# Node products moved ahead of the sums, and the sums dealt out by a tile quota, in a one-core graph kernel

## The chip, the cores and the metric

The kernel runs on one core of one Trainium2 chip. The metric is the device time of one execution in microseconds (us); lower is better. A core has five engines that take their instructions in order from queues of their own: PE (matmuls; its weight loads are listed apart as PEld), DVE and ACT (elementwise work), POOL (here almost only the issue of indirect DMAs) and SP (here the issue of plain DMAs). Line numbers such as L1353 are those of the kernel before the change.

## The reference, cut to what matters

N = 6250 nodes with 64 features, 206,250 edges (sorted by `dst`). Every edge gives a hidden row, rows are summed by node, and each node's mean goes through a small network and a layer norm:

```
msg = concat([x[dst], edge_attr])              # per edge, 128
h   = relu(msg @ W1a.T + b1a) @ W1b.T + b1b    # per edge
agg = segment_sum(h, src) / max(count, 1)      # per node
z   = relu(concat([x, agg]) @ W2a.T + b2a) @ W2b.T + b2b
out = concat([z, x]) @ Wr.T + br
y   = layernorm(x + out)
```

The second edge layer is linear, so the kernel sums `relu(...)` (128 values and a count) and applies W1b to the sums.

## The kernel before, in words

`fast_path` does all the work here; `general_path` is a second program behind a flag and does not run with these inputs.

**Blocks.** The edges are padded to 1612 tiles of 128 and taken in 124 blocks of 13 tiles (`NG`), in an order that strides through the array so that every block spreads over all nodes. The main loop (`for k, ep_ in enumerate(epoch_of)`) runs block by block. The nodes are cut into 49 bins of 128 (`NB`). In block k, PE computes the hidden rows of the block's edges (`hidden`, L1313), ACT applies the relu into one of four row buffers (`orow`, L1316), and the ranks of the edges in their bins are worked out for a later block on PE, DVE and ACT (`bins_of`, `counts_of`, `slots`), so that each row gets a slot of its own in DRAM.

**Scatters.** `scatter(k - LEAD)`, two blocks later, has POOL issue one indirect DMA (L1353) for each tile of 128 rows. In blocks 8 to 103 (`JOIN_FROM`, `JOIN_TO`) six of the 13 tiles are joined: two joins turn three tiles each into rows of four ("quads") by one-hot matmuls (`marks` on DVE L1201 and on ACT L1206 and L1207, `join` L1233, `join_rows` L1246), and each join is one indirect DMA (L1324). So such a block has 7 + 2 = 9 scatters, and each of the other 28 blocks has 13: 1228 in all. A table in `scatter` (`pace`) makes some scatters of block k wait for matmuls of block k + 2. The row buffers close the circle: ACT's copy of the low bits into the buffer (L1626, at the head of each block) waits until earlier scatters have read it.

**Sums.** Rows go to four DRAM buffers by epoch (blocks 0 to 103, 104 to 115, 116 to 119, 120 to 123), and the quads to one more. A slot range that is surely full can be read back while later blocks still run: a `Step` is the range of tiles [lo, hi) of all bins together with the block `at` which it is full. `FULL = (4, 8, 12)` and `FULLQ = (4, 8, 11)` set these ranges. `groups_of` cuts a step into groups of at most 3 bins and 12 tiles. A group is read by SP (`read`, L1415, into nine buffers, `READS`), DVE makes its one-hot tiles (`nodes_of`, L1444; this is done ahead, when the group before it is finished, by `mark`), PE sums it with one matmul of two passes per tile (`summed`, L1463), and the result is added into `part` (DVE L1523; the first time ACT copies it, L1521). In block k the first group that was issued in an earlier block is summed half ahead of the last part of the hidden rows and half after the joins; further groups follow at the end of the block. If no group was issued in the block before, nothing has been marked ahead.

**The plan before.** The groups of a step are spread evenly over the blocks from `at + LATE` (4 later) to the next step's `at + LATE`. Worked out from the constants, that is 0 or 12 tiles a block from block 34, mixed 0, 12 and 24 up to block 99, 30 to 42 in blocks 100 to 107, 44 in blocks 108 to 118, about 60 in blocks 119 to 123, and 98 after the last block. The last epoch's 98 tiles are summed in the final stage.

**Products over x.** Two products per node, -(x W2a + b) and the residual with its bias, do not depend on the sums. `load_x` reads x into SBUF in block 106 (`top.x`, in the memory that the joins have left), and `nodes_ahead` (L1585 to L1595) computes four bins in each of the blocks 109 to 121 (`PRE`), in place, into `zT` and `xr`.

**Final stage.** After the last block come the rest of the sums, then 17 groups of the last epoch, each followed in a software pipeline by mean, transpose, layer, residual and norm (`Nodes`). It needs the products of all bins.

**Order.** PE, ACT, DVE and SP run in the order of the program text (`manual_schedule`); POOL's order is the framework's.

## Time and profile before

| | us |
|---|---|
| median of three runs | 1736.17 |
| the three runs | 1719.88, 1737.81, 1736.17 |
| the profiled execution | 1717.97 |
| its span from first to last instruction | 1716.2 |
| busy: PE, DVE, POOL, ACT | 1486.7, 1312.5, 1184.8, 1067.1 |
| mean granted PE clock | 0.944 |

The profile is one execution. A row of the groups reads: line, engine, operation, output <- input, count | busy time and mean ns of one | idle time of the engine just before, and what ended most of it. A row of the timeline reads: start, duration, engine, line, what, count (merged if next to each other), and in brackets the engine's idle time before it and what ended that. A row of the windows gives for a stretch of time the busy time and instruction count of PE, PEld, DVE, ACT and POOL, the granted clock, the busy share of the 16 DMA engines and their GB/s.

### The profile page before, as it was taken

The page shows a single profiled execution, that of the slowest core. Times are in us where ns is not written, and L with a number is a line of the kernel's source. Part 1 is how long each engine was busy: PE and PEld are TensorE (multiplying, and loading weights), DVE is VectorE, ACT ScalarE, POOL GpSimd, SP SyncE. Part 2 cuts the span into 40 slices and gives each one's busy share as a digit, 9 for nine tenths or more (in the row PEclk, how much of TensorE's full clock was granted, in tenths as well). Part 3 has the DMA queues.
Part 4 walks back from the last instruction along what each step waited for, and adds up shares of the span by engine and source line. Part 5 has one row for each costly group of instructions (what it writes and reads, how often), then busy time and mean ns, then how long its engine had stood idle before and what let it go on. Part 6 is the DMA issues. An engine that isn't in the chain of part 4 may idle for free.

```text
span 1716.2 us, 32843 instructions
## 1 busy us (share of the span) xinstructions
PE 1486.7 (87%) x10851; PEld 1347.6 (79%) x10851; DVE 1312.5 (76%) x3024; ACT 1067.1 (62%) x2161; POOL 1184.8 (69%) x1244
## 2 busy tenths in 40 slices
PE   5846777787788899898999899999998999999997
PEld 4835666566677788887888889888988889899986
DVE  8454666676767788798799898899986767677787
ACT  2246778887676878688688777777654343433026
POOL 5777777777776777677677777677657777776700
PEclk9687899989898999999899999999999899999999
DMA  7865777766566778687678688788989999897982
GB/s 184 255 216 189 227 244 249 246 213 198 180 192 198 219 224 255 204 242 221 209 216 264 207 242 266 224 253 248 287 242 300 276 257 274 253 268 255 311 253 51
DMA packets 222097, 399.41 MB, mean 233 GB/s; under 512 B 43283, under 2 KB 121799, under 8 KB 221663
## 3 DMA queue, kind: packets, MB, share of 16 engines
q1 hardware_dynamic: 134317, 221.51, 47.0%
q0 software_dynamic: 48512, 120.15, 20.2%
q10 hardware_dynamic: 39090, 55.56, 9.5%
q8 instruction: 88, 1.44, 0.4%
q14 instruction: 90, 0.74, 0.1%
HBM read 219.56 MB, written 177.48 MB: 231 GB/s over the span
## 4 chain that ended last, share of the span: by engine, by line
PE 49%; ACT 16%; DMA 10%; DVE 6%; issue 4%; POOL 1%; SPq 0%; ACTq 0%; DVEq 0%; POOLq 0%
PE h_ps L1463 25%; PE h_ps L1233 7%; PE h_ps L1313 7%; DMA rows<-orow,rowidx 6%; PE h_ps L1246 4%; ACT marks L1206 3%; ACT rhs L1284 3%; ACT marks L1207 3%; DMA quads<-orow,qidx 2%; ACT orow L1316 2%; DMA rt<-rows 2%; DVE oh L1444 1%; ACT rhs L1286 1%; ACT rj L1238 1%; ACT orow L1249 1%
## 5 line engine op out<-in xcount | busy, mean ns | idle before, releaser
L1353 POOL DMA_INDIRECT rows<-orow,rowidx x1036 | 997.6, 963 | 383.7 <-issue 188.8
L1463 PE MATMUL h_ps<-rt,oh 128*128 128x129 f32 x4204 | 526.3, 283 | 57.1 <-ACT rhs L1284 49.2
L1463 PEld LDWEIGHTS h_ps<-rt,oh 128*128 128x128 f32 x4204 | 504.4, 198 | 59.5 <-ACT rhs L1284 50.5
L1316 ACT ACTIVATE orow<-h_ps 128x384 f32<-128x384 f32 (+1 forms) x304 | 160.2, 530 | 310.8 <-PE h_ps L1313 302.0
L1444 DVE TENSOR_TENSOR oh<-ramp,rt 128x512 f32<-128x512 bf16 (+3 forms) x452 | 327.9, 768 | 14.7 <-DMA rt<-rows 14.4
L1233 PE MATMUL h_ps<-marks,side 128*128 128x512 f32 x1152 | 302.1, 410 | 37.2 <-ACT marks L1207 37.2
L1313 PE MATMUL h_ps<-mv,rhs 124*128 124x128 f32 x2072 | 293.7, 288 | 2.2 <-issue 2.0
L1233 PEld LDWEIGHTS h_ps<-marks,side 128*128 128x128 f32 x1152 | 214.0, 195 | 86.2 <-ACT marks L1207 44.8
L1313 PEld LDWEIGHTS h_ps<-mv,rhs 124*128 124x128 f32 x2072 | 272.9, 204 | 7.5 <-issue 3.6
L1246 PEld LDWEIGHTS h_ps<-mv,rj 128*128 128x128 f32 x1536 | 199.6, 199 | 93.8 <-ACT rj L1238 68.4
L1246 PE MATMUL h_ps<-mv,rj 128*128 128x130 f32 x1536 | 213.4, 292 | 67.3 <-ACT rj L1238 52.7
L1201 DVE TENSOR_TENSOR marks<-quad_ramp,ramp 128x1024 fp32r<-128x1024 f32 x192 | 225.6, 1213 | 3.9 <-PE h_ps L1233 3.7
L1324 POOL DMA_INDIRECT quads<-orow,qidx x192 | 184.9, 963 | 58.8 <-issue 16.8
L1238 ACT COPY rj<-h_ps 128x512 f32<-128x512 f32 x192 | 109.3, 589 | 95.6 <-PE h_ps L1233 94.3
L1222 DVE TENSOR_TENSOR side<-enat,side 128x384 fp32r<-128x384 f32 x96 | 53.6, 558 | 133.1 <-ACT side L1215 133.0
L1016 DVE TENSOR_TENSOR_SCAN had<-ramp,bins 128x400 bf16<-128x400 bf16 (+1 forms) x124 | 139.0, 1121 | 8.6 <-ACT bins L1037 6.3
L1207 ACT ACTIVATE marks<-marks,ones 128x512 fp32r<-128x512 f32 x192 | 138.7, 722 | 6.3
L1206 ACT ACTIVATE marks<-quad_ramp,z_act 128x512 fp32r<-128x512 f32 x192 | 136.8, 712 | 0.0
L1284 ACT ACTIVATE rhs<-rhs,from_win 60x896 f32<-60x896 bf16 (+1 forms) x116 | 133.2, 1148 | 2.9
L1286 ACT ACTIVATE rhs<-rhs,ones 60x896 f32<-60x896 f32 (+1 forms) x116 | 133.1, 1148 | 2.9
L1523 DVE TENSOR_TENSOR part<-part,h_ps 128x258 f32<-128x258 f32 (+2 forms) x201 | 95.3, 474 | 46.9 <-PE h_ps L1463 46.5
L1249 ACT ACTIVATE orow<-h_ps 128x260 f32<-128x260 f32 x384 | 121.3, 391 | 12.7 <-PE h_ps L1246 10.0
(180 smaller groups left out, 1457.6 us busy)
## 6 DMA issues: line engine op xcount, KB each, us to landing
rt<-rows SPq DMA_DIRECT2D x146, 260.0 KB
rt<-rows SPq DMA_DIRECT2D x80, 390.0 KB
rt<-quads SPq DMA_DIRECT2D x96, 260.0 KB
rhs<-in_edgeT SPq DMA_DIRECT2D x96, 224.0 KB
enat<-in_edgeJ SPq DMA_DIRECT2D x96, 192.0 KB
rows<-orow,rowidx POOLq DMA_INDIRECT x1036
rt<-quads SPq DMA_DIRECT2D x49, 325.0 KB
rows<-padrow ACTq DMA_DIRECT2D x12, 1300.0 KB
```

The source lines that it names most:

```text
L1201: nc.vector.tensor_tensor(m[:, :n, :], all_q[:, None, :].to_broadcast([P, n, QUAD * P]), z[:, :n, None].to_broadcast([P, n, QUAD * P]), op ...
L1206: nc.scalar.activation(m[:, t, :], all_q, AF.Square, bias=z_acts[k][:, i * JOIN + t : i * JOIN + t + 1], scale=-1.0)
L1207: nc.scalar.activation(m[:, t, :], m[:, t, :], AF.Relu, bias=ones[:, :1], scale=-1.0)
L1233: nc.tensor.matmul(ps, s[:, p, i * JOIN + t, :], m[:, t, :], start=t + p == 0, stop=t == JOIN - 1 and p == 1,)
L1246: done[k, f"join{i}"] = nc.tensor.matmul(ps[:, j, :], rj[:, (g0 + j) * P : (g0 + j + 1) * P], m, start=True, stop=True).ins.name
L1284: nc.scalar.activation(of_win, rel, AF.Square, bias=from_win[D:WIDE, :])
L1313: done[k, c] = nc.tensor.matmul(ps[:, j, :], rhs[:WIDE, of * P : (of + 1) * P], m[:WIDE, :H], start=True, stop=True).ins.name
L1316: nc.scalar.activation(orow_of(k, k0, n)[:, :, :H], ps[:, :n, :], AF.Relu)
L1324: s = nc.gpsimd.indirect_dma_start(out=qep.rows.rearrange("(q r) f -> q (r f)", r=QUAD), out_offset=bass.IndirectOffsetOnAxis(ap=qidx[:, q ...
L1353: s = nc.gpsimd.indirect_dma_start(out=ep_.rows, out_offset=bass.IndirectOffsetOnAxis(ap=rowidx[:, k % RING * BLK + j : k % RING * BLK + j ...
L1444: nc.vector.tensor_tensor(res[:, at_tile : at_tile + nb * n, :], ramp[:, None, :].to_broadcast([P, nb * n, P]), node[:, :, None].to_broadc ...
L1463: m = nc.tensor.matmul(of_bin(b), oh[:, at_tile, :], rt[:, j * n + t, : H + 1], start=t0 + t == st.lo[b], stop=t0 + t == st.hi[b] - 1,)
```

## The change

- The steps become `FULL = (2, 6, 10, 12)` and `FULLQ = (2, 6, 10)`. The first two full tiles of every bin are ready at block 13 (before: the first four, at block 29).
- All groups stand in one queue in order of readiness, and each block takes groups until its quota of tiles (`RATES`: 50 for a block without joins, 13 for one with two) is used up; an overdraft counts against the next block. What is left after the last block is taken then.
- The products over x are made in every second block from 9 to 33, from a small tile of x for four bins (`xin`, loaded by SP a block earlier) into small tiles (`nz`, `xr_now`), and stored to DRAM by SP a block later (`nqs`, `xrs`). Block 106 loads the two results (4.8 MB) in place of x (1.6 MB).
- The copy of the low bits, and the memset beside it, move from the head of the block to just ahead of the hidden rows: on ACT behind the four activations of `marks`.
- The assertion on order and the loop after the last block are rewritten to match.

```diff
--- before.py
+++ after.py
@@ -454,14 +454,15 @@
 NEAR = 8
 Y_AHEAD = 32
 HEAD = 117
-FULL = (4, 8, 12)
+FULL = (2, 6, 10, 12)
 BIG = 2.0**20
 LATE = 4
 BUFS = 4
 RD = 6
 SUMS, TILES = 3, 12
 SEG = 9
-PRE = 109
+PRE, EVERY = 9, 2
+RATES = {0: 50, 2: 13, 3: 9}
 RING = 8
 ROWS, EDGES, READS = 4, 4, 9
 SPREAD = 4.8
@@ -474,7 +475,7 @@
 JOINS = 3 if THRICE else 2
 SIDES, ENATS = 2, 3
 ON_ACT = 1
-FULLQ = (4, 8, 11)
+FULLQ = (2, 6, 10)
 
 
 def order_of(ngr):
@@ -661,6 +662,8 @@
     qep.rows = dram.tile([(NQ + NREST) * QUAD, W], F32, name="quads")
     relt = dram.tile([NGR, NG * P], BF16, name="relt")
     ytab = dram.tile([NB * P, H], F32, name="ytab")
+    nqs = dram.tile([P, NB * P], F32, name="nqs")
+    xrs = dram.tile([P, NB, D], F32, name="xrs")
 
     by_edge = ctx.enter_context(ExitStack())
     ep = by_edge.enter_context(tc.tile_pool(name="fedge", bufs=1))
@@ -795,6 +798,10 @@
             t.sides = [t.tile([P, 2, JT, P], F32R, f"side{i}") for i in range(SIDES)]
             t.enats = [t.tile([P, JT, D], F32, f"enat{i}") for i in range(ENATS)]
             t.rjs = [t.tile([P, QUAD * P], F32, f"rj{i}") for i in range(2)]
+            t.xin = t.tile([P, SUB * P], F32, "xin")
+            t.nz = t.tile([P, SUB * P], F32, "nz")
+            t.xr = t.tile([P, SUB, D], F32, "xr_now")
+            nc.vector.tensor_copy(t.xin[D : D + 1, :].rearrange("o (b p) -> o b p", p=P), ones[D : D + 1, None, :].to_broadcast([1, SUB, P]))
             for side in t.sides:
                 nc.vector.tensor_copy(side[:, 0, :, WIDE], ones[:, :JT])
                 for part_of, c0 in ((0, WIDE + 1), (1, D)):
@@ -835,6 +842,12 @@
             )
             nc.sync.dma_start(zT[:D, :half], xT[:, :half])
             nc.sync.dma_start(zT[:D, half:N], xT[:, half:])
+
+        def load_nodes():
+            half = NB // 2
+            for b in (slice(0, half), slice(half, NB)):
+                nc.sync.dma_start(nq[:, b.start * P : b.stop * P], nqs[:, b.start * P : b.stop * P])
+                nc.sync.dma_start(xr[:, b, :], xrs[:, b, :])
 
         def load_dst():
             nc.sync.dma_start(at_i, first.rearrange("(g o) -> g o", o=1))
@@ -1302,6 +1315,14 @@
         made = {}
 
         done = {}
+
+        def low_bits(k):
+
+
+            j0 = JOIN * joined(k)
+            if k >= ROWS and j0 < JOIN * joined(k - ROWS):
+                nc.vector.memset(orow_of(k, j0, JOIN * joined(k - ROWS) - j0)[:, :, H], 1.0)
+            nc.scalar.copy(orow_of(k, j0, BLK - j0)[:, :, H + 1], lo[:, k * BLK + j0 : (k + 1) * BLK])
 
         def hidden(k, parts):
             rhs, _, m = made[k]
@@ -1547,13 +1568,17 @@
 
         epoch_of = [ep_ for ep_ in epochs for _ in range(ep_.end - ep_.first)]
 
-        groups_at = [[] for _ in range(NGR + LATE)]
-        for sts in (steps, [*qep.steps, epochs[1].steps[-1]]):
-            for st, after in zip(sts, sts[1:]):
-                grs = groups_of(st)
-                n = after.at - st.at
-                for i in range(n):
-                    groups_at[st.at + LATE + i] += [(st, g) for g in grs[i * len(grs) // n : (i + 1) * len(grs) // n]]
+        groups_at, queue, credit = [[] for _ in range(NGR + 1)], [], 0
+        for k in range(NGR + 1):
+            for st in (*steps[:-1], *qep.steps):
+                if k == min(st.at + LATE, NGR):
+                    queue += [(st, g) for g in groups_of(st)]
+            credit += RATES[joined(k)] if k < NGR else len(queue) * TILES
+            while queue and credit > 0:
+                st, g = queue.pop(0)
+                credit -= sum(nb * n for _, nb, _, n in g)
+                groups_at[k].append((st, g))
+            credit = min(credit, 0)
         to_issue = []
 
         def issue(k):
@@ -1578,21 +1603,38 @@
             nc.vector.tensor_scalar(mean, mean, -1.0 / D, None, op0=ALU.mult)
             nc.vector.tensor_scalar(w, w, mean, None, op0=ALU.add)
 
+        def nodes_cols(b0):
+            n = min(SUB, NB - b0)
+            return n, slice(b0 * P, (b0 + n) * P)
+
+        def nodes_load(b0):
+            n, cols = nodes_cols(b0)
+            have = min(N, cols.stop) - cols.start
+            if have < n * P:
+                nc.vector.memset(top.xin[:D, have : n * P], 0.0)
+            nc.sync.dma_start(top.xin[:D, :have], xT[:, cols.start : cols.start + have])
+
         def nodes_ahead(b0):
-            n = min(SUB, NB - b0)
-            cols = slice(b0 * P, (b0 + n) * P)
+            n, cols = nodes_cols(b0)
+            xin, nz, xr = top.xin, top.nz, top.xr
             qp = hp.tile([P, SUB * P], F32, name="h_ps")
-            nc.tensor.matmul(qp[:, : n * P], w2x_t, zT[: D + 1, cols], start=True, stop=True)
+            nc.tensor.matmul(qp[:, : n * P], w2x_t, xin[: D + 1, : n * P], start=True, stop=True)
             xp = hp.tile([P, 2, SUB, D], F32, name="h_ps")
             for j in range(n):
-                b = slice((b0 + j) * P, (b0 + j + 1) * P)
-                nc.tensor.matmul(xp[:, 0, j, :], zT[: D + 1, b], wrx_t, start=True, stop=True)
-            nc.vector.tensor_scalar(zT[:, cols], qp[:, : n * P], -1.0, None, op0=ALU.mult)
-            nc.scalar.copy(xr[:, b0 : b0 + n, :], xp[:, 0, :n, :])
+                nc.tensor.matmul(xp[:, 0, j, :], xin[: D + 1, j * P : (j + 1) * P], wrx_t, start=True, stop=True)
+            nc.vector.tensor_scalar(nz[:, : n * P], qp[:, : n * P], -1.0, None, op0=ALU.mult)
+            nc.scalar.copy(xr[:, :n, :], xp[:, 0, :n, :])
             for j in range(n):
-                b = slice((b0 + j) * P, (b0 + j + 1) * P)
-                nc.tensor.matmul(xp[:, 1, j, :], zT[:, b], nwzz_t, start=True, stop=True)
-            nc.vector.tensor_add(xr[:, b0 : b0 + n, :], xr[:, b0 : b0 + n, :], xp[:, 1, :n, :])
+                nc.tensor.matmul(xp[:, 1, j, :], nz[:, j * P : (j + 1) * P], nwzz_t, start=True, stop=True)
+            nc.vector.tensor_add(xr[:, :n, :], xr[:, :n, :], xp[:, 1, :n, :])
+
+        def nodes_store(b0):
+            n, cols = nodes_cols(b0)
+            nc.sync.dma_start(nqs[:, cols], top.nz[:, : n * P])
+            nc.sync.dma_start(xrs[:, b0 : b0 + n, :], top.xr[:, :n, :])
+
+        nodes_at = {PRE + EVERY * i: b0 for i, b0 in enumerate(range(0, NB, SUB))}
+        assert JOIN_FROM - 3 < PRE - 1 and max(nodes_at) < JOIN_TO
 
         in_order = ctx.enter_context(ExitStack())
         in_order.enter_context(
@@ -1621,14 +1663,12 @@
             after = joined(k + 1) if k + 1 < NGR else 0
             if k + 2 < NGR and k > 0:
                 carried(k + 2)
-            if k >= ROWS and j0 < JOIN * joined(k - ROWS):
-                nc.vector.memset(orow_of(k, j0, JOIN * joined(k - ROWS) - j0)[:, :, H], 1.0)
-            nc.scalar.copy(orow_of(k, j0, BLK - j0)[:, :, H + 1], lo[:, k * BLK + j0 : (k + 1) * BLK])
             for i in range(joined(k)):
                 marks(k, i)
             if k == 1:
                 join_consts()
             if k == 0:
+                low_bits(k)
                 hidden(k, ((0, 4), (4, 3), (7, 3), (10, 3)))
                 window(1)
                 columns(1)
@@ -1640,6 +1680,7 @@
                 carried(k + 2)
             *parts, last_part = {0: ((0, 4), (4, 3), (7, 3), (10, 3)), 2: ((6, 4), (10, 3)), 3: ((9, 4),)}[joined(k)]
             if k > 0:
+                low_bits(k)
                 hidden(k, parts)
             if after:
                 join_bases(k + 1)
@@ -1648,8 +1689,8 @@
                 window(k + 2)
             if k == JOIN_TO + 2:
                 top = last_top()
-                zT, xr = top.x, top.xr
-                load_x()
+                nq, xr = top.x, top.xr
+                load_nodes()
             if k == NEAR - 6:
                 load_x()
                 load_dst()
@@ -1698,8 +1739,12 @@
                 nc.vector.tensor_add(wrx_t[D:, :], wrx_t[D:, :], wps[D : D + 1, H:])
                 nc.vector.tensor_add(wrx_t[:D, :], wrx_t[:D, :], ident[:D, :D])
                 centred(wrx_t)
-            if 0 <= k - PRE < -(-NB // SUB):
-                nodes_ahead((k - PRE) * SUB)
+            if k in nodes_at:
+                nodes_ahead(nodes_at[k])
+            if k - 1 in nodes_at:
+                nodes_store(nodes_at[k - 1])
+            if k + 1 in nodes_at:
+                nodes_load(nodes_at[k + 1])
             if k in clears:
                 clear(*clears[k])
             issue(k)
@@ -1737,17 +1782,15 @@
                 places_in_windows()
         for k in range(NGR - LEAD, NGR):
             scatter(k)
-        for k in range(NGR, NGR + LATE):
-            to_issue += groups_at[k]
-            issue(k)
-            while issued or marked:
-                sum_next(k)
-                issue(k)
+        to_issue += groups_at[NGR]
+        issue(NGR)
+        while issued or marked:
+            sum_next(NGR)
+            issue(NGR)
 
 
         last = steps[-1]
         NF = N // P
-        nq = zT
         with tc.tile_pool(name="nw2", bufs=2) as nw2, tc.tile_pool(name="nw", bufs=3) as nw:
 
             class Nodes:
```

## The prediction

> **What bounds the kernel now.** First the groups of instructions on the page, for the engine that never rests; then the waits, for what interrupts it.
>
> ```profile
> span 1716.2 us, 32843 instructions
> L1353 POOL DMA_INDIRECT rows<-orow,rowidx x1036 | 997.6, 963 | 383.7 <-issue 188.8
> L1463 PE MATMUL h_ps<-rt,oh 128*128 128x129 f32 x4204 | 526.3, 283 | 57.1 <-ACT rhs L1284 49.2
> L1324 POOL DMA_INDIRECT quads<-orow,qidx x192 | 184.9, 963 | 58.8 <-issue 16.8
> L1523 DVE TENSOR_TENSOR part<-part,h_ps 128x258 f32<-128x258 f32 (+2 forms) x201 | 95.3, 474 | 46.9 <-PE h_ps L1463 46.5
> ```
> ```profile
> ACT orow L1316 <- PE h_ps L1313: 302.0, 119, 12.6
> POOL rows L1353 <- issue: 188.8, 616, 0.8
> ACT orow L1626 <- DMA rows<-orow,rowidx: 72.7, 21, 10.6
> PE h_ps L1463 <- ACT rhs L1284: 49.2, 12, 4.9
> POOL rows L1353 <- DVE rhs L1291: 13.9, 1, 13.9
> ```
>
> PE is 87% busy, and the longest single sum in the waits is ACT's, but the thread is POOL. A scatter takes 0.963 us and the next follows after 0.306 (188.8 over 616): 1.27 us each, 11.4 for a block of nine, 16.5 for one of thirteen. All 1228 take 1182.5 us busy and 376 of such gaps. POOL's idle time is 383.7 + 58.8 = 442.5; less 376 and the 13.9 before the first scatter, **53 us** are left in which POOL waited for somebody. That, and what follows the last scatter, is all that the change can shorten:
>
> ```profile
> 1599.80 2.17 PE L1313 MATMUL h_ps<-mv,rhs 124*128 124x128 f32 x18
> 1626.91 0.96 POOL L1353 DMA_INDIRECT rows<-orow,rowidx  x1 [0.30 <-issue]
> 1654.93 2.92 PE L1463 MATMUL h_ps<-rt,oh 128*128 128x129 f32 x24 [1.31 <-issue]
> ```
>
> The last scatter ends at 1627.9. The last epoch's sums need it, yet start only at 1654.9, since PE is still at older sums; from there the final stage takes 61.3. So the tail is 88.3 us, 27 of them older sums.
>
> Where the 53 come from is seen in the timeline around two neighbouring blocks, 36 without sums and 37 with one group:
>
> ```profile
> 451.08 0.33 PE L1058 MATMUL cnt_ps<-had,one_w 128*128 128x400 bf16 x1
> 453.42 0.92 PE L1313 MATMUL h_ps<-mv,rhs 124*128 124x128 f32 x6
> 455.52 0.56 DVE L1222 TENSOR_TENSOR side<-enat,side 128x384 fp32r<-128x384 f32 x1 [0.67 <-ACT side L1215]
> 459.58 0.33 PE L1058 MATMUL cnt_ps<-had,one_w 128*128 128x400 bf16 x1
> 465.35 1.88 DVE L1444 TENSOR_TENSOR oh<-ramp,rt 128x512 f32<-128x512 bf16 x3
> 466.14 3.78 PE L1463 MATMUL h_ps<-rt,oh 128*128 128x129 f32 x16 [4.06 <-ACT rhs L1284]
> 476.96 0.33 PE L1058 MATMUL cnt_ps<-had,one_w 128*128 128x400 bf16 x1
> 546.59 0.96 POOL L1353 DMA_INDIRECT rows<-orow,rowidx  x1 [1.36 <-PE h_ps L1313]
> 550.68 0.96 POOL L1353 DMA_INDIRECT rows<-orow,rowidx  x1 [1.86 <-PE h_ps L1246]
> 554.41 2.03 PE L1463 MATMUL h_ps<-rt,oh 128*128 128x129 f32 x16
> 743.53 0.24 ACT L1626 CAST orow<-lo 128x7 f32<-128x7 bf16 x1
> 809.27 0.20 ACT L1626 CAST orow<-lo 128x7 f32<-128x7 bf16 x1 [0.70 <-DMA quads<-orow,qidx]
> ```
>
> Without sums a block takes 8.5 us. One whose sums follow an idle block takes 17.4: nothing was marked ahead, DVE makes the one-hot tiles late, PE waits 4.06 and sums slowly (16 matmuls in 3.78 us, against 2.03 later). Such an unready block is the row of 12 in the waits. The pair takes 25.9, POOL's two blocks 22.8. Three such pairs pass without a wait of POOL (a lead of some 3 x 3.1 = 9 us is used up); near 546 POOL waits 1.36 and 1.86. Blocks with 12 tiles each time hold: blocks 60 to 66 took 65.7 us, 10.96 each, under POOL's 11.4.
>
> **The change: the plan.** From the constants, sums restart after an idle block only in blocks 18, 32, 50 and 81 instead of 12 times. From 50 to 104 most blocks have 12 tiles, seven 24, and single 24s are covered by the lead. So nearly all of the 53 us go; block 50's overrun (17.4 - 11.4 = 6) fits the lead of 9, and I keep 2 for block 81. The two-tile steps give 228 groups for 218 and 429 reads for 452; ten more additions at 0.474 us lie on DVE beside POOL's scatters, and if DVE were late they would cost 4.7.
>
> **The products, leaving.** In blocks 109 to 121 they lengthen PE's block:
>
> ```profile
> 1519.86 0.25 ACT L1626 CAST orow<-lo 128x13 f32<-128x13 bf16 x1
> 1528.58 1.02 PE L1585 MATMUL h_ps<-x_late,w2x_t 65*128 65x512 f32 x2
> 1531.42 1.10 PE L1594 MATMUL h_ps<-nwzz_t,x_late 128*128 128x64 f32 x8 [0.98 <-ACT xr L1591]
> 1532.36 1.56 PE L1463 MATMUL h_ps<-rt,oh 128*128 128x129 f32 x12
> 1537.03 0.26 ACT L1626 CAST orow<-lo 128x13 f32<-128x13 bf16 x1
> ```
>
> The block takes 17.17 us, and 1532.36 - 1528.58 = 3.78 of that are the products, their wait included. Without them 13.4. A tile costs 526.3/2102 = 0.25, so six more (50 for 44) make 14.9, under POOL's 16.5. PE then keeps its lead instead of losing 0.7 a block, and the older sums can run while POOL finishes.
>
> **The products, arriving.**
>
> ```profile
> L1590 DVE TENSOR_SCALAR x_late<-h_ps 128x512 f32<-128x512 f32 x12 | 8.3, 691 | 38.9 <-PE h_ps L1589 38.9
> ```
>
> Thirteen times, at 9, 11, ... 33. PE's own part is 1532.36 - 1528.58 less the wait of 0.98 before L1594: 2.8. The wait is for DVE, which negates the first product (L1590) only behind L1222, 5.0 us into block 36 (455.52 + 0.56 - 451.08). PE has its ranks done 2.3 into it (453.42) and the first two products 1.9 later, at 4.2; DVE's negation takes 0.69 from 5.0 on. So PE waits 1.5, between the 0.98 seen late and the 4.06 of the unready block, and nearer the former, since it stands behind one long step less than L1444. A block with products then takes 8.5 + 2.8 + 1.5 = 12.8, a pair with a bare one 21.3 of POOL's 22.8: free, covered by POOL; if that cover goes, 4.3 a block. With sums it isn't free. Pairs 19/20, 21/22 and 33/34 take 12.8 + 3.0 (12 tiles) + 10.96 = 26.8, 4.0 over; 23/24, with 18 tiles, 5.5; 17/18 and 31/32, whose second block is unready, 12.8 + 17.4 = 30.2, 7.4. Together 32, less the lead of 9: **23 us** of new waits of POOL. Low end 0: the lead refills between 26 and 31, and DVE and ACT overlap. High end: a wait of 4.06 each time and products at half pace make 8.5 + 5.6 + 4.1 = 18.2 a block, so 3.9 over in 7 pairs without sums, 9.4 in three, 10.9 in one and 12.8 in the two unready ones: 92 - 9 = 83.
>
> The clock is in that end. PE's eight L1594 matmuls took 1.97 us at 1357, after a wait for reads, and 1.10 above.
>
> ```profile
> 1326.92 0.69 DVE L1444 TENSOR_TENSOR oh<-ramp,rt 128x512 f32<-128x512 bf16 x1 [9.60 <-DMA rt<-rows]
> 1356.96 1.97 PE L1594 MATMUL h_ps<-nwzz_t,x_late 128*128 128x64 f32 x8 [0.90 <-ACT xr L1591]
> ```
>
> The Trainium skill, TensorE: Matmul & The Clock Gate, Part 1 (What's actually happening), says that the array falls to half clock after an idle window of about 3.4 us. By that rule a wait of 1.5 leaves the clock alone, the 4.06 before L1463 doesn't, and the trace agrees (3.78 against 2.03 for 16 matmuls); were each wait of the products past it, the sum would be the slow end.
>
> **The copy of the low bits.** ACT waited there 72.7 us in 21 blocks; now the four `marks` run before that wait. ACT isn't on POOL's path while POOL is the bound, so 0; where PE is late it doesn't wait there at all. Ends: 0 and a few us of lead. Nothing else queues behind it that didn't.
>
> **SP.** 39 more small DMAs and four large ones in place of three.
>
> ```profile
> 1309.76 0.51 SPq L836 DMA_DIRECT2D x_late<-in_xT  x1
> 1310.32 0.59 SPq L837 DMA_DIRECT2D x_late<-in_xT  x1
> ```
>
> At half a microsecond each the small ones are 1.5 us per pair of blocks on a queue that waits for buffers. A store waits for DVE's last addition of the block before, which precedes matmuls that SP waits for anyway to reload the edges: 0, and if SP were late, edges and reads behind it would be.
>
> **The load in block 106** puts 4.8 MB ahead of the reads, where 1.6 were.
>
> ```profile
> 1360.00:1556.00 196.00, 185.21 (x1550) 176.57 (x1550) 139.92 (x227) 71.37 (x101) 148.74 (x156) 0.99 0.89 257
> 1603.00:1654.00 51.00, 49.95 (x441) 49.27 (x440) 41.62 (x67) 0.49 (x1) 19.08 (x20) 1.00 0.97 310
> ```
>
> At 310 GB/s 3.2 MB more are 10 us. Before, DVE waited 9.60 for a read just behind x, and POOL lost nothing, as PE's lead covered it. Now twice that: 5 of POOL's time (ends 0 and 10). The DMA engines are 89% busy at 44 tiles a block; 50 tiles add 0.4 MB to 257 GB/s x 17.2 us = 4.4; at 289 to 320 GB/s (257/0.89 and 310/0.97) that is 15.1 to 16.7 us of a block of 16.5: full, hardly past it.
>
> The Trainium skill, DMA: Bandwidth & Descriptors (Issuing engines are not separate DMA queues), says that DMAs of all queues run on the same 16 engines and interleave. That speaks against the change, as POOL's scatters would share in the crowding; it is the second rival below.
>
> **The tail.** 142 tiles are left after block 123 instead of 98. With its lead, PE is done with block 123 some 45 us before the last scatter (three blocks of 16.5, less its own work), has 50 + 142 tiles left, 48 us, and, with the DMA engines near full and 10 us behind, ends about 14 after it, not 27. Tail 14 + 61.3 = 75. Ends: 88, and 68 if nothing older is left; of the 7 us then between, 2.55 are a scatter's landing and the rest an estimate for a read and the one-hot tiles:
>
> ```profile
> 263.41 0.96 POOL L1353 DMA_INDIRECT rows<-orow,rowidx  x1 [0.30 <-PE h_ps L1246]
> 266.92 0.20 ACT L1626 CAST orow<-lo 128x7 f32<-128x7 bf16 x1 [1.62 <-DMA rows<-orow,rowidx]
> ```
>
> **Sum.** POOL's waits 53 -> 23 + 2 + 5 = 30: -23. Tail 88 -> 75: -13. Together -36 of the profiled execution's 1717.97 us (span 1716.2 and 1.8 around it): 1682. The median of the runs is 18 above that execution, so I predict **1700** for the median; the times of the rivals include these 18 too. With w for the new early waits it is 1736 - 53 + w + 7 - 13 = 1677 + w.
>
> **Rivals.**
> 1. Slower: early blocks with products stall as an unready block does. It decides from w = 59 on (no gain), and from 76 on it is slower by over 1%; at the high end, w = 83, the time is **1760**. For it: the unready block's 4.06 and 3.78 are of the same form, PE behind DVE. Against it: L1590 is one short instruction, where L1444 takes 1.88 first.
> 2. The late blocks become bound by the DMA engines: the load costs its full 10, and 44 more older tiles behind the last scatter (2.9 MB at 310 GB/s, 9 us) make the tail 97. 1700 + 5 + 22 = **1727**. For it the 89 to 97% above and 83 more tiles from block 104 on (1103 for 1020); against it that POOL lost nothing there before.
> 3. The products are hidden under sums too: w = 0 and a tail of 68. 1677 - 7 = **1670**.
>
> **The numbers.** Mine 0.42, rival 3 0.16, rival 2 0.22, rival 1 0.20. A measurement of this kernel tells about 1% from no change. Mine and rival 3 are faster by more: 0.58; rival 2 is within it: 0.22; rival 1 is slower: 0.20. Mine alone is 1680 (w = 10, tail 68) to 1720 (w = 36, tail 82). The range takes in rivals 3 and 2 and the lower half of rival 1's way: 1660 to 1742.
>
> **What would show it.** POOL's idle time falls from 442 to about 420; the waits near 546 vanish, and new ones stand between 190 and 460, with the matmuls of the hidden rows and of `join_rows` as releasers; PE's wait before the last product is near 1.5; blocks 108 to 119 keep 16.5; the last epoch's sums start some 14 us after the last scatter. I am wrong if POOL's waits in blocks 9 to 40 pass 50 us or are under 10, or if late blocks pass 17 us on reads.

## The result, and the profile after

The changed kernel takes 1682.88 us (median of four runs, 1679.46 to 1686.59) where the kernel before takes 1736.99 beside it (median of four, 1719.88 to 1749.84): a ratio of 0.9721, 95% interval 0.9647 to 0.9794. That ratio leaves out the run of 1749.84, which lies over 1.5% above the shortest of its kernel and counts as slow. The profiled execution took 1686.59 us (span 1684.6). In later runs the kernel before stood at 1719.69 (median of 18, 1714.18 to 1747.59); against that the gain is 37 us. Seven of the twelve experiments below (e5 to e11), on three chips, met a TensorE that was held back: its matmuls started late with nothing to wait for (the traces are shown at e11), and the kernel before took 2144 to 2179 us. Those runs are told by themselves.

The groups of the page after; L1374, L1345 and L1484 are the L1353, L1324 and L1463 of before:

```profile
span 1684.6 us, 32855 instructions
...
L1374 POOL DMA_INDIRECT rows<-orow,rowidx x1036 | 1002.3, 968 | 363.2 <-issue 179.2
...
L1484 PE MATMUL h_ps<-rt,oh 128*128 128x129 f32 x4204 | 520.2, 280 | 37.1 <-ACT rhs L1297 19.6
...
L1345 POOL DMA_INDIRECT quads<-orow,qidx x192 | 185.2, 964 | 59.4 <-issue 21.9
```

And its waits (engine, line, awaited: us in total, times, longest):

```profile
ACT orow L1325 <- DMA rows<-orow,rowidx: 211.2, 33, 13.0
...
POOL rows L1374 <- issue: 179.2, 588, 0.3
...
POOL rows L1374 <- PE h_ps L1334: 23.6, 36, 4.8
POOL rows L1374 <- PE h_ps L1259: 23.1, 41, 2.4
...
PE h_ps L1484 <- ACT rhs L1297: 19.6, 4, 8.0
...
PE h_ps L1484 <- DVE oh L1465: 16.2, 1, 16.2
```

A scatter costs nearly what it cost (968 and 964 ns for 963 and 963), but over 1228 of them that is 1187.5 us for 1182.5, 5 us more. POOL's idle time is 363.2 + 59.4 = 422.6 for 442.5. PE's waits in unready blocks are 19.6 us in 4 for 49.2 in 12: the plan restarts the sums four times. ACT's wait for the copy of the low bits grew from 72.7 to 211.2. A longer row of an engine that is off the path need not cost anything: in e3 this wait grew to 106.6 and the time did not change.

The timeline, where the new waits stand: the product of block 23 with sums behind it, and POOL's waits at that time, in the scatters of block 22; the load in block 106; the last scatter; and the first sum of the last epoch.

```profile
321.03 1.90 PE L1628 MATMUL h_ps<-nwzz_t,nz 128*128 128x64 f32 x8 [0.91 <-ACT xr_now L1626]
322.72 1.61 PE L1484 MATMUL h_ps<-rt,oh 128*128 128x129 f32 x6
...
326.31 0.96 POOL L1374 DMA_INDIRECT rows<-orow,rowidx  x1 [4.77 <-PE h_ps L1334]
...
330.92 0.96 POOL L1374 DMA_INDIRECT rows<-orow,rowidx  x1 [2.38 <-PE h_ps L1259]
...
1314.96 0.96 DVE L1465 TENSOR_TENSOR oh<-ramp,rt 128x768 f32<-128x768 bf16 x1 [16.61 <-DMA rt<-rows]
...
1323.84 0.96 POOL L1374 DMA_INDIRECT rows<-orow,rowidx  x1 [6.18 <-ACT orow L1337]
...
1612.12 0.96 POOL L1374 DMA_INDIRECT rows<-orow,rowidx  x1 [0.30 <-issue]
...
1623.42 2.92 PE L1484 MATMUL h_ps<-rt,oh 128*128 128x129 f32 x24 [1.31 <-issue]
```

To see where time went, what each gap of POOL has beyond 0.31 us is put to the block of its scatter, in all traces in which TensorE ran free. It is worked out from POOL's rows of the timelines. All in us; the start of 16 to 17 us in block 0 is left out.

| kernel | POOL's waits, blocks 8-39 | 40-103 | 104-107 | 108-123 | last scatter ends | tail after it | span |
|---|---|---|---|---|---|---|---|
| before | 0.1 | 47.9 | 0.2 | 6.0 | 1627.9 | 88.3 | 1716.2 |
| before, second trace (e12) | 0.2 | 44.7 | 0.5 | 29.2 | 1650.1 | 88.4 | 1738.5 |
| after | 28.9 | 0.0 | 5.9 | 0.0 | 1613.1 | 71.5 | 1684.6 |
| e1, new plan alone | 2.1 | 0.6 | 0.3 | 25.2 | 1601.7 | 89.2 | 1690.9 |
| e2, early products alone | 12.9 | 45.2 | 0.0 | 0.0 | 1632.4 | 76.9 | 1709.3 |
| e3, low bits alone | 0.0 | 42.0 | 0.4 | 5.7 | 1625.0 | 88.3 | 1713.3 |
| e4, before with early marks | 0.0 | 13.7 | 0.3 | 21.1 | 1611.1 | 88.4 | 1699.5 |

### The profile page after: what moved, and what is told of

It reads as the page before. It is cut to its first block, busy times and chain, and to the rows that moved or that the text cites. A ratio compares the mean times of both kernels' runs of the same rounds, so it can differ in the third digit from the quotient of the medians.

```text
span 1684.6 us, 32855 instructions
## 1 busy us (share of the span) xinstructions
PE 1472.0 (87%) x10851; PEld 1341.5 (80%) x10851; DVE 1321.5 (78%) x3017; ACT 1060.5 (63%) x2161; POOL 1189.8 (71%) x1244
## 4 chain that ended last, share of the span: by engine, by line
PE 47%; DMA 17%; ACT 13%; DVE 12%; issue 5%; POOL 4%; ACTq 1%; DVEq 0%; POOLq 0%; SPq 0%
PE h_ps L1484 21%; DMA rows<-orow,rowidx 13%; PE h_ps L1246 8%; PE h_ps L1334 6%; PE h_ps L1259 4%; POOL rows L1374 3%; DVE oh L1465 2%; DMA quads<-orow,qidx 2%; ACT orow L1262 2%; DMA rt<-rows 2%; ACT rhs L1299 2%; DVE marks L1214 2%; ACT rhs L1297 2%; ACT orow L1337 2%; ACT marks L1219 1%
## 5 line engine op out<-in xcount | busy, mean ns | idle before, releaser
L1374 POOL DMA_INDIRECT rows<-orow,rowidx x1036 | 1002.3, 968 | 363.2 <-issue 179.2
L1484 PE MATMUL h_ps<-rt,oh 128*128 128x129 f32 x4204 | 520.2, 280 | 37.1 <-ACT rhs L1297 19.6
L1484 PEld LDWEIGHTS h_ps<-rt,oh 128*128 128x128 f32 x4204 | 497.9, 196 | 38.2 <-ACT rhs L1297 20.0
L1465 DVE TENSOR_TENSOR oh<-ramp,rt 128x512 f32<-128x512 bf16 (+2 forms) x429 | 327.7, 802 | 45.2 <-DMA rt<-rows 31.5
L1334 PE MATMUL h_ps<-mv,rhs 124*128 124x128 f32 x2072 | 294.8, 289 | 19.5 <-ACT orow L1337 17.5
L1246 PEld LDWEIGHTS h_ps<-marks,side 128*128 128x128 f32 x1152 | 218.9, 197 | 43.4 <-ACT orow L1337 0.9
L1345 POOL DMA_INDIRECT quads<-orow,qidx x192 | 185.2, 964 | 59.4 <-issue 21.9
L1325 ACT CAST orow<-lo 128x7 f32<-128x7 bf16 (+1 forms) x124 | 24.2, 195 | 236.9 <-DMA rows<-orow,rowidx 211.2
L1544 DVE TENSOR_TENSOR part<-part,h_ps 128x387 f32<-128x387 f32 (+2 forms) x211 | 103.6, 492 | 60.7 <-PE h_ps L1484 60.1
```

Source lines behind the costliest of these rows:

```text
L1246: nc.tensor.matmul(ps, s[:, p, i * JOIN + t, :], m[:, t, :], start=t + p == 0, stop=t == JOIN - 1 and p == 1,)
L1334: done[k, c] = nc.tensor.matmul(ps[:, j, :], rhs[:WIDE, of * P : (of + 1) * P], m[:WIDE, :H], start=True, stop=True).ins.name
L1345: s = nc.gpsimd.indirect_dma_start(out=qep.rows.rearrange("(q r) f -> q (r f)", r=QUAD), out_offset=bass.IndirectOffsetOnAxis(ap=qidx[:, q ...
L1374: s = nc.gpsimd.indirect_dma_start(out=ep_.rows, out_offset=bass.IndirectOffsetOnAxis(ap=rowidx[:, k % RING * BLK + j : k % RING * BLK + j ...
L1465: nc.vector.tensor_tensor(res[:, at_tile : at_tile + nb * n, :], ramp[:, None, :].to_broadcast([P, nb * n, P]), node[:, :, None].to_broadc ...
L1484: m = nc.tensor.matmul(of_bin(b), oh[:, at_tile, :], rt[:, j * n + t, : H + 1], start=t0 + t == st.lo[b], stop=t0 + t == st.hi[b] - 1,)
```

## The experiments

The theory: the end is POOL's 1228 scatters, plus POOL's waits, plus the tail. The plan takes the waits of blocks 40 to 103 away; the products bring new ones where they stand under sums, and their leaving the late blocks shortens the tail. The first rival: the late blocks are bound by the DMA engines, so that the products' place doesn't matter. The second: a product costs about the same wherever it stands. e1 to e4 undo or do one part alone; the kernel before has a median of 1719.69 beside them.

### e1: the new plan alone

The kernel before with the two-tile steps and the quota; the products stay at blocks 109 to 121.

```diff
-FULL = (4, 8, 12)
+FULL = (2, 6, 10, 12)
...
+RATES = {0: 50, 2: 13, 3: 9}
...
-FULLQ = (4, 8, 11)
+FULLQ = (2, 6, 10)
...
-                    groups_at[st.at + LATE + i] += [(st, g) for g in grs[i * len(grs) // n : (i + 1) * len(grs) // n]]
+            credit += RATES[joined(k)] if k < NGR else len(queue) * TILES
+            while queue and credit > 0:
```

> The kernel before with the new steps and the tile quota alone; the products stay in blocks 109 to 121. My theory (time is POOL's scatters, plus POOL's waits, plus the tail): nearly no waits of POOL up to block 104 (0 to 5 us), but 50 tiles and the products make 18.7 us of PE in thirteen late blocks against POOL's 16.5, so some 15 us of late waits and a tail of 95 or more: span about 1693, some 23 below before. Rival (the plan is all of the gain): span 1685, as with the whole change. Rival (the products' move is all of it): span 1716, as before.

Measured: 1692.12 us, ratio 0.9808 (0.9758 to 0.9858), with a span of 1690.9 where the theory had 1693. The parts are off both ways: late waits of 25.2 for some 15, a tail of 89.2 for 95 or more. By the table the waits of blocks 40 to 103 go, 47.9 to 0.6. But 25.2 stand in blocks 112 to 121 (6.0 in the late blocks before), where 50 tiles and a product share a block. A row of POOL's timeline there, block 114:

```profile
1427.83 0.96 POOL L1354 DMA_INDIRECT rows<-orow,rowidx  x1 [5.17 <-ACT orow L1317]
```

ACT there waits for PE's hidden rows: PE has lost its lead. The tail stays at 89.2. So the plan is worth 27.6 us, and of the 47 that it saves early it loses 19 late, as long as the products are there. Part of these 19 is half clock, which e12 explains.

### e2: the early products alone

The changed kernel with the old steps, the old even dealing and the low bits at their old place.

```diff
-FULL = (2, 6, 10, 12)
+FULL = (4, 8, 12)
...
-FULLQ = (2, 6, 10)
+FULLQ = (4, 8, 11)
...
+            low_bits(k)
             for i in range(joined(k)):
                 marks(k, i)
...
```

> The kernel before with the products moved to blocks 9 to 33 and through DRAM, old plan of sums, old place of the low bits. My theory: under no sums the products cost POOL next to nothing (0 to 4 us in blocks 9 to 33), the waits of blocks 40 to 103 stay (about 48), the load in block 106 costs about 5, and PE's lead in the late blocks brings the tail from 88 to some 70: span about 1702. Rival (each of the thirteen costs POOL 2 us, with or without sums): 26 us more in blocks 9 to 33, span about 1725.

Measured: 1712.13 us, ratio 0.9923 (0.9886 to 0.9959), with a span of 1709.3, 7 above what the theory gave. The late waits go (6.0 to 0.0) and the tail falls by 11.4, which rules out the rival that the products' place doesn't matter. The early waits, 12.9, lie between the theory's 0 to 4 and the 26 of the rival recorded above, so neither was right: blocks 18 to 28 cost 5.9 with no sum near them, and blocks 34 to 38, which found no lead left (PE was no longer ahead of POOL), another 7.0. The last matmuls of a product (L1624) come there in PE's timeline as follows; the other rows are the same steps of PE in a block with a product and in the bare block behind it.

```profile
290.27 1.10 PE L1624 MATMUL h_ps<-nwzz_t,nz 128*128 128x64 f32 x8 [2.23 <-ACT xr_now L1622]
291.21 1.31 PE L1334 MATMUL h_ps<-mv,rhs 124*128 124x128 f32 x6
292.18 4.26 PE L1246 MATMUL h_ps<-marks,side 128*128 128x512 f32 x12
...
300.45 0.91 PE L1334 MATMUL h_ps<-mv,rhs 124*128 124x128 f32 x6
301.12 2.99 PE L1246 MATMUL h_ps<-marks,side 128*128 128x512 f32 x12
305.62 2.05 PE L1259 MATMUL h_ps<-mv,rj 128*128 128x130 f32 x16 [1.50 <-ACT rj L1251]
...
314.01 1.10 PE L1624 MATMUL h_ps<-nwzz_t,nz 128*128 128x64 f32 x8 [2.22 <-ACT xr_now L1622]
...
337.76 1.10 PE L1624 MATMUL h_ps<-nwzz_t,nz 128*128 128x64 f32 x8 [2.23 <-ACT xr_now L1622]
```

The products come every 23.74 us, while POOL's two blocks take 22.8: 0.9 a pair, which is what POOL waits in each of the blocks 20, 22, 24 and 26. So a pair with a product isn't free even without sums. The other rows show one reason: behind the product the same 12 matmuls take 4.26 us for 2.99, and the granted clock is 0.50 from 291.50 to 294.92.

Both parts on one kernel show what each does for the other: alone they cost 2.1 and 12.9 in blocks 8 to 39, together 28.9; in blocks 108 to 123 the plan alone costs 25.2, with the products gone 0.0, and the tail is 71.5 instead of 89.2.

### e3: the low bits alone

The kernel before with `low_bits` ahead of the hidden rows.

```diff
-            nc.scalar.copy(orow_of(k, j0, BLK - j0)[:, :, H + 1], lo[:, k * BLK + j0 : (k + 1) * BLK])
...
+                low_bits(k)
                 hidden(k, parts)
```

> The kernel before with only the copy of the low bits moved behind marks. My theory: 0, span 1716 within 5, POOL's waits about 53. Rival (marks ahead of the wait give PE up to 2.9 us more lead in each block): POOL's waits fall by 10 or more, span about 1703.

Measured: 1718.23 us, ratio 1.0009 (0.9963 to 1.0054): no difference, as expected.

### e4: the kernel before, with marks made earlier

If a block sums for the first time after a pause, its first one-hot tiles are made earlier within that block: right behind `join_bases` and the first lane side, ahead of DVE's work for the next blocks.

```diff
                 side(k + 1, 0)
+            if due > 0 and not marked:
+                mark()
```

> The kernel before with one line more: in a block whose sums were not marked ahead, DVE makes the one-hot tiles behind join_bases instead of behind all its work for the next blocks. My theory (the unready block costs because PE waits for DVE): PE's 4 us waits before the sums shrink to under 1, an unready block from 17.4 to about 13.5, POOL's waits from 53 to about 35, span about 1698. Rival (the block is long because of its tiles or the read, not the marking): waits and span stay, 1716.

Measured: 1694.53 us, ratio 0.9816 (0.9757 to 0.9875). From block 8 to 98 POOL doesn't wait any more, 34 us less: the unready blocks were the cause, and two lines cure them without a new plan. But blocks 117 to 121 cost 21.1, more than the 6.0 of before. So the theory's 35 us of waits came out (35.1) by luck: more was won early, and some lost late. The windows show why (20 us each; the last three columns are the granted clock, the DMA share, GB/s):

```profile
1420.00:1440.00 20.00, 19.02 (x164) 18.23 (x164) 15.33 (x33) 6.25 (x9) 15.12 (x17) 1.00 0.88 268
...
1480.00:1500.00 20.00, 19.02 (x135) 18.23 (x134) 12.24 (x24) 6.23 (x9) 13.48 (x15) 0.83 0.80 236
```

PE is as busy in both, but does 135 matmuls for 164, at a clock of 0.83. The four runs fall apart likewise, 1688 and 1689 at mean clocks of 0.957 and 0.954, 1700 and 1701 at 0.948 and 0.951. e12 takes that up.

### e5 to e8: further than the change

Four edits of the changed kernel: e5 puts the products where the new plan has no sums,

```diff
-        nodes_at = {PRE + EVERY * i: b0 for i, b0 in enumerate(range(0, NB, SUB))}
+        nodes_at = dict(zip(CLEAR_OF_SUMS, range(0, NB, SUB)))
...
+CLEAR_OF_SUMS = (7, 9, 11, 13, 15, 26, 28, 30, 40, 42, 44, 46, 48)
```

> The changed kernel with its thirteen products put at blocks 7, 9, 11, 13, 15, 26, 28, 30, 40, 42, 44, 46 and 48, where the new plan has no sums (its sums run in blocks 17 to 24, 31 to 38 and from 49). Theory (a product costs POOL time only where it stands under sums): the changed kernel's 28.9 us of POOL's waits before block 40 fall to 2 to 7 (with the new plan and no early products at all they were 2.0; with early products and no sums, 6.3 in blocks 18 to 28), nothing else moves, the tail stays near 71.5: span 1684.6 - 25 = 1660, median 1658, between 1654 and 1664. Rival (a product costs about 2 us of POOL wherever it stands): the waits stay at 25 or more and the median at 1679 to 1684. Second rival (PE is the bound behind block 104, so what POOL wins early comes back as waits in blocks 108 to 121 or as a longer tail): early waits of 2 to 7, but a median over 1668.

e6 loads the products in 26 pieces,

```diff
-                load_nodes()
+            if 0 <= k - JOIN_TO - 4 < -(-NB // SUB):
+                load_nodes(k - JOIN_TO - 4)
```

> The changed kernel with the 4.8 MB that block 106 loads in four DMAs split into 26 DMAs, two in each of blocks 108 to 120. Theory (the load is late for nobody, it only stands ahead of a read): DVE's and PE's waits of 16.6 and 16.2 us for one read go, POOL's 5.9 in block 106 goes, the tail stays or gains up to 3 us: span 1676 to 1679, median 1674 to 1677. Rival (the late blocks are bound by the DMA engines, so that the same bytes cost the same wherever they stand): POOL's waits turn up in blocks 108 to 120 or in the tail, median 1680 to 1686.

e7 puts the low bits back to the head of the block,

```diff
+            low_bits(k)
             for i in range(joined(k)):
                 marks(k, i)
```

> The changed kernel with the copy of the low bits back at its old place in the block, ahead of the marks. Theory (the copy's place matters little): the old kernel with this one edit changed its median by 0.1%, and here too it is within 5 us, 1678 to 1688, with the early waits at 26 to 34. Rival (the move gave PE's lead in the blocks that hold a product and sums): early waits over 38 and a median over 1693.

and e8 is e5, e6 and the early marks of e4 together (here too the tiles are made earlier within the block, not a block earlier).

> The changed kernel with the products clear of the sums, the load in pieces, and in the three blocks that sum for the first time after a pause one read's one-hot tiles made a block earlier, right behind the lane sides. Theory (POOL's waits are the only cost that is left ahead of the last scatter, and they add up): 35 us of waits become 0 to 4, the last scatter ends at 1580, the tail is 69 to 72: span 1651, median 1646 to 1654. Rival (PE is the bound behind block 104): the early gain is given back by waits in blocks 108 to 121, as it was with the old kernel whose marks were made early (21 us in blocks 117 to 121), or by a longer tail: median 1660 or more.

Measured: 2205.36, 2209.58, 2213.68 and 2204.18 us, with the kernel before at 2178.84: ratios of 1.015 (1.007 to 1.023), 1.018 (1.010 to 1.026), 1.020 (1.012 to 1.028) and 1.018 (1.009 to 1.027). No theory had that, since all four were reckoned from POOL, and here PE sets the end. They differ among themselves by 0.4%, less than their intervals. Of the questions that they were made for, they settle none.

### e9, e10 and e11: the same once more, and the change itself

e9 is e5's kernel and e10 is e8's, unaltered; e11 is the changed kernel, unaltered.

> The kernel with the products clear of the sums once more, since on the chip of its first run TensorE was held back for hundreds of microseconds and set the end of every kernel. Where the kernel before runs at about 1720, the expectation is the old one: early waits of 2 to 7 in place of 28.9, median 1654 to 1664 (a product costs POOL time only under sums); 1679 to 1684 if a product costs the same anywhere; over 1668 with few early waits if PE is the bound behind block 104. Where the kernel before runs near 2180 again, TensorE is the bound and the median is 2195 to 2215.

> The kernel with products clear, load in pieces and early marks once more. Where the kernel before runs at about 1720: 35 us of POOL's waits become 0 to 4 and the tail is 69 to 72, median 1646 to 1654; 1660 or more if PE gives the gain back behind block 104. Where the kernel before runs near 2180 again, TensorE is the bound and the median is 2195 to 2215.

> The changed kernel itself once more, unaltered, against the kernel before on one chip. Where the kernel before runs at about 1720 (TensorE free): 1676 to 1690, as in the first measurement. Where it runs near 2170 (TensorE held back): the four kernels of the last runs that share the new plan and the early products were 1.5 to 2.0% slower than the kernel before there, so if these two parts are the cause it is 2195 to 2215, a ratio of 1.01 to 1.02; the rival, that only the added edits of those kernels lose time there and the change itself still gains, gives a ratio under 1.

Measured: 2204.58 and 2209.53 with the kernel before at 2169.6, ratios of 1.017 (1.009 to 1.025) and 1.017 (1.009 to 1.026); then 2174.1 with the kernel before at 2144.0, a ratio of 1.0133 (1.0075 to 1.0190). The first two are what was expected for that case; e11's ratio is in the expected 1.01 to 1.02, its median below the expected 2195 to 2215, as the kernel before was faster there too. So while TensorE is held back the change itself is slower, by 1.3%. e11 ran on the chip of e1 to e4, where the kernel before had taken 1720 some 23 minutes earlier, so it isn't a matter of which chip. What holds TensorE back no run shows. The page of e11, its span and what the engines were busy, against 1472.0, 1321.5, 1060.5 and 1189.8 of PE, DVE, ACT and POOL after:

```profile
span 2167.0 us, 32855 instructions
...
PE 1668.4 (77%) x10851; PEld 1479.3 (68%) x10851; DVE 1324.3 (61%) x3017; ACT 1067.0 (49%) x2161; POOL 1195.1 (55%) x1244
```

Only PE works much longer, by 196 us, and it is idle for longer too. A large part of that idle time waits for nothing that the profile shows, as the waits of the sums' matmuls tell, first after, then e11:

```profile
PE h_ps L1484 <- issue: 1.3, 1, 1.3
```
```profile
PE h_ps L1484 <- issue: 124.7, 160, 5.3
```

Blocks 108 to 123 by the windows, first of the trace after, then of e11:

```profile
1350.00:1613.00 263.00, 251.95 (x2183) 248.67 (x2182) 205.20 (x325) 75.28 (x106) 199.60 (x209) 0.98 0.95 304
```
```profile
1669.00:2060.00 391.00, 291.95 (x1902) 264.60 (x1902) 179.91 (x284) 79.64 (x110) 195.78 (x205) 0.78 0.60 180
```

and PE's timeline of e11 in one of them:

```profile
1781.62 1.50 PE L1484 MATMUL h_ps<-rt,oh 128*128 128x129 f32 x12
1782.96 0.83 PE L1334 MATMUL h_ps<-mv,rhs 124*128 124x128 f32 x6
1783.63 5.42 PE L1484 MATMUL h_ps<-rt,oh 128*128 128x129 f32 x47
1789.89 0.49 PE L1484 MATMUL h_ps<-rt,oh 128*128 128x129 f32 x3 [0.84 <-issue]
1791.30 0.51 PE L1484 MATMUL h_ps<-rt,oh 128*128 128x129 f32 x3 [0.92 <-issue]
1792.04 0.27 PE L1484 MATMUL h_ps<-rt,oh 128*128 128x129 f32 x1 [0.23 <-issue]
1793.44 0.48 PE L1484 MATMUL h_ps<-rt,oh 128*128 128x129 f32 x2 [1.13 <-issue]
1794.16 0.27 PE L1484 MATMUL h_ps<-rt,oh 128*128 128x129 f32 x1 [0.24 <-issue]
```

47 matmuls pass at full pace, then PE starts one to three at a time, about 0.7 or 1.4 us from one start to the next, though their inputs are there (issue). That is how a held-back TensorE looks here: gaps of one spacing, put down to nobody, and most where PE has most to do (blocks 108 to 123 take 391 us for 263, 1.49 times as long, the whole span 1.29 times).

### e12: the kernel before, for its trace

> The kernel before, unaltered, for its trace in the state in which TensorE is held back and the changed kernel runs at 2174 and this one at 2144. In that state the changed kernel's stages are longer than in its first trace by 1.23 (blocks 8 to 33, 402 for 326), 1.23 (34 to 48, 211 for 172), 1.25 (49 to 103, 786 for 631), 1.38 (104 to 107) and 1.49 (108 to 123, 391 for 263). The same factors on this kernel's first trace (296, 180, 667, 66, 267 and a tail of 89) would give about 2190, so some 45 us must be missing in a stage. Theory A (without sums and products the blocks 8 to 33 keep POOL's pace): that stage is under 330. Theory B (the late blocks, with 44 tiles for 50, are held back less): blocks 108 to 123 are under 360. Theory C: the difference lies in blocks 49 to 103, under 790. If TensorE is free in this run, the span is 1712 to 1746 and the trace tells nothing of it.

Measured: 1740.27 us (one run; another of the same kernel beside it 1729.7). TensorE was free, so it can't say where the 30 us of e11 arise; its theories A to C stay untried. But it is 22 us longer than the first trace of the very same kernel, and shows where. By the table both reach block 108 alike, with waits of 48 and 45 us before it; all of the 22 lie behind. The windows of the late blocks, first trace, then e12, and then a product of each:

```profile
1360.00:1627.00 267.00, 254.09 (x2162) 244.97 (x2162) 194.17 (x327) 81.48 (x118) 197.90 (x208) 0.99 0.89 266
```
```profile
1360.00:1627.00 267.00, 254.10 (x1964) 245.00 (x1964) 178.80 (x298) 81.21 (x118) 180.44 (x189) 0.91 0.81 239
```
```profile
1497.09 1.10 PE L1594 MATMUL h_ps<-nwzz_t,x_late 128*128 128x64 f32 x8 [0.98 <-ACT xr L1591]
1498.03 1.56 PE L1463 MATMUL h_ps<-rt,oh 128*128 128x129 f32 x12
```
```profile
1470.30 1.88 PE L1594 MATMUL h_ps<-nwzz_t,x_late 128*128 128x64 f32 x8 [0.98 <-ACT xr L1591]
1471.97 2.89 PE L1463 MATMUL h_ps<-rt,oh 128*128 128x129 f32 x12
```

The wait ahead of the product is 0.98 us in both. In the first trace the matmuls behind it keep their pace (8 in 1.10, 12 in 1.56); in e12 they take 1.88 and 2.89, and from this product to the next it is 20.4 us instead of 17.2. PE had 0.7 us a block too little even before; with 1.6 to 3.3 more behind eight of the products its lead is gone by block 114, where POOL waits (3.8).

Why behind one wait of 0.98 and not behind the next? In these traces the granted clock is either 1.00 or 0.50, and it changes only at the ends of steps of 3.41 us that run on through the whole execution. Four such steps of e12; the wait of 0.98 shown last lies at the end of the first of them, the matmuls behind it in the second and third:

```profile
1467.02:1470.43 3.41, 2.43 (x17) 1.81 (x16) 0.69 (x1) 3.00 (x4) 2.63 (x3) 1.00 1.08 236
1470.43:1473.85 3.42, 3.42 (x17) 3.42 (x18) 1.52 (x5) 0.00 (x0) 2.50 (x4) 0.50 0.73 199
1473.85:1477.26 3.41, 3.41 (x18) 3.41 (x18) 3.41 (x5) 1.05 (x2) 2.52 (x3) 0.50 0.46 96
1477.26:1480.67 3.41, 3.41 (x32) 3.41 (x32) 1.92 (x4) 1.56 (x3) 2.78 (x3) 1.00 0.72 226
```

The five traces with late products (before, e1, e3, e4, e12) hold 56 waits of 0.98 us ahead of one. In the 20 that began 0.67 to 2.47 us into a step, the next step ran at 0.50; in the 36 that began at 2.56 to 3.34 or 0.02 to 0.63, it ran at 1.00. In the first trace a block takes 17.17 us, five steps and 0.10, so that each wait begins 0.10 later in its step than the one before: the first of them began at 2.85 and the last at 0.42, and none met the bad part. In e12 they began at 0.47, 0.57 and 0.67, and from there the clock fell; a block of 20.44 us is six steps less 0.04, which held the next four in the bad part (2.40, 2.35, 2.31, 2.26). So with a product in a block in which PE is the limit, the time hangs on where the first product meets these steps, which is luck.

The run times fit that, if loosely: the two kernels whose products are early lie within 3 us (e2, nine runs, clock 0.932 to 0.936) and 7 us (after, four runs); of the 18 runs of the kernel before, 15 lie within 17.5 us and three up to 33 above the shortest, with clocks from 0.946 in the shortest to 0.924 in the longest, and e3 ranges over 26.5. But e1, with late products, lies within 6.4 in its four runs.

## Why the prediction was right, and where it was not

- **The plan.** 53 us of waits from block 40 on were to shrink to 2 in block 81 and the load's 5. They did: 47.9 in blocks 40 to 103 became 0.0, and e1 (0.6) shows that it is the plan's doing. The 6.0 of the late blocks went with the products (e2).
- **The products, arriving: 23 forecast, 28.9 measured.** That they cost more where they stand under sums was right, since e1 and e2 cost 2.1 and 12.9 and both together 28.9. Two things were off. A pair with a product and no sums was reckoned at 21.3 us and called free; e2 has 23.74. Of these 2.4, 0.7 is PE's wait, 2.23 for 1.5. The prediction put it down to DVE's negation, but it is ACT's copy that ends it, as its own row said (0.98 <-ACT xr L1591): in the change 12 of the 13 waits, 31.7 us, end with ACT's copy and one with DVE's. Another 0.7 is half clock in the step of 3.41 us behind the product (from its end to the ranks of the next block 6.9 us, for 6.16 in block 36), and 0.9 is PE's wait for ACT in the bare block, 1.50 for the 0.61 of block 36, from which the 8.5 was read. And with sums too, half clock, which the forecast kept for its slow end, did come in part: in block 23 the eight product matmuls took 1.90 us, where they took 1.10 without it, and six sum matmuls 1.61; POOL's largest waits on PE, 4.77 and 2.38, stand beside it.
- **The load: 5 forecast, 5.9 measured**, with 16.6 us of DVE's waiting for "twice 9.60".
- **The tail: 75 forecast, 71.5 measured.** PE is 10.3 us behind the last scatter (1623.4 less 1613.1), not 14; the final stage takes 61.2. e2 shows that the products' leaving does most of it (76.9), and e1 that the plan alone doesn't (89.2).
- **Low bits, SP, late blocks.** 0 each, as forecast: e3 for the first, in the kernel before; POOL loses nothing in blocks 108 to 123 with the DMA engines at 0.95 and 304 GB/s, so the second rival, which had 27 us for them, is out. The first rival needed 59 us of early waits and the third none; both are out by the 28.9.
- **The sum.** For the profiled execution the terms gave 1682, and 1686.6 was measured. The waits are 34.8 for 30 (from 54.2 by the table, where the sum had 53), and the scatters themselves are 5.0 longer, for which the sum had no term; the tail is 3.5 shorter. That it comes so close is partly luck, as the tail makes up for some of the rest.
- **The step that failed is "The median of the runs is 18 above that execution, so I predict 1700".** It took the distance of one execution from a median of three for something that every kernel's median has. In 18 later runs the kernel before has a median of 1719.69, only 1.7 above the 1717.97, so most of the 18 was the chance of three runs. What scatters them is seen in e12 for one long execution: half clock behind the products in the late blocks, or none. The change takes the products out of there; its median, 1682.88, is 3.7 below its profiled execution. So the 36 that were forecast are met by the 37 against the later runs, but not by the 54 against those beside it.

Open: whether clear products, pieces and early marks win the 35 us that the table still shows (28.9 early, 5.9 at the load), as e5, e6 and e8 never met a free TensorE; why a wait counts in one part of a step and not in another; and why the changed kernel is 1.3% slower than before when TensorE is held back, since no trace of before exists from such a time.

## What to carry to other kernels

Find the engine that never rests and write the time as its work, its waits by stage and what follows it; then a change that moves work is priced by the lead that the feeding engine has at the old place and at the new one, and two moves that meet in a block cost more than their sum. A lead that is won early is only kept if the later stages have slack: e1 and e4 gave back some 15 to 19 us in blocks where PE was the limit. And when runs of one program spread, compare a short and a long trace of it stage by stage before taking the difference for an offset.

## What the runs showed of the hardware

- **The clock fell behind a wait of 0.98 us in 20 cases of 56, by where the wait began in a step of 3.41 us** (e12; the steps run on through the execution, and the clock granted in each is 1.00 or 0.50). A fall can also come just too late to be seen beside its wait. Two products of the changed kernel without sums near them:

```profile
164.72 1.97 PE L1628 MATMUL h_ps<-nwzz_t,nz 128*128 128x64 f32 x8 [3.27 <-ACT xr_now L1626]
...
189.79 1.10 PE L1628 MATMUL h_ps<-nwzz_t,nz 128*128 128x64 f32 x8 [2.23 <-ACT xr_now L1626]
```

  Behind the 3.27 the eight matmuls take 1.97. Behind the 2.23 they pass at full pace, but the clock falls 1.6 us later: it is 0.50 from 191.4 to 194.8. The Trainium skill, TensorE: Matmul & The Clock Gate, Part 1 (What's actually happening), puts the fall to half clock at an idle window of about 3.4 us, of a window that runs freely and so meets a program differently from run to run. The steps of 3.41 us and the change from run to run agree with it; the falls behind 0.98 us, four products in a row in e12, do not, and here the measurement decides.
- **TensorE was held back in every run of three sessions, on three chips within twelve minutes**, to matmuls started some 0.7 us apart, with the other engines at their usual pace (DVE busy 1324 us for 1322, POOL 1195 for 1190). The kernels before and after then stand at 2144 and 2174 us, in the other order (ratio 1.0133, 1.0075 to 1.0190, for 0.9721). It isn't bound to a chip: that of e11 had been free 23 minutes earlier. The gain of this change, which lies in POOL's waits and the tail, was not there in such a time.
